# Where the first state of a chunk reads its step product, and how the first token groups are convolved

## The chip, the cores and the metric

One core of a Trainium2 chip. The engines are called by their names in the profile: PE (TensorE, with its weight loads as PEld), DVE (VectorE), ACT (ScalarE), POOL (GpSimd) and SP (SyncE, which issues the DMAs). The metric is the device time of one launch in microseconds; the time before is the median of 3 runs. All data is float32.

## The reference, cut to what matters

Two layers, each with a "conv" part and an "ffn" part. The change touches the first part alone, a two-dimensional selective scan over 4 images of 64x64 tokens with 128 channels. Four directions `k`, 256 inner channels (two halves of 128) and 16 states per channel:

```python
xc = silu(depthwise_conv3x3(xh) + conv_b)          # xh: half of x @ in_proj_w.T
xs = [x0, x1, x0 reversed, x1 reversed]            # x1: columns instead of rows
dts, Bm, Cm = split(einsum('bkdl,kcd->bkcl', xs, x_proj_weight))
delta = softplus(einsum('bkrl,kdr->bkdl', dts, dt_projs_weight) + dt_projs_bias)
...
def step(h, xs):
    ut, dt, bt, ct = xs
    dA = jnp.exp(dt[..., None] * A)
    h = dA * h + (dt * ut)[..., None] * bt[:, :, None, :]
    y = jnp.einsum('bkdn,bkn->bkd', h, ct)
    return (h, y)
```

After it come the norm, the gate and the output projection, then a mixture of experts over tokens, and a second layer with a self/row/column mixing and a spectral (FFT) convolution.

## The kernel before

**The scan.** The 4096 tokens of an image are cut into 8 chunks of 512, so there are 4 images x 4 directions x 8 = 128 chunks, and each has N = 16 states: 2048 states in all, in the loop over `s`, with `i` the chunk and `n` the state in it. For every state, channels lie on the 128 partitions, the two halves `h` behind one another:

- SP loads `bc`, the rows of B and C of that state, broadcast over the partitions, 5 states ahead (`bufs=6`).
- ACT makes `da`, the exponential of the step size times A, one instruction for each half, 3 states ahead (`bufs=5`).
- DVE multiplies the step product (step size times input) by B's row into `db[h]`, a PSUM tile of one buffer for each half, and scans: `hh = da * h + db` along the tokens.
- POOL copies the last column of `hh` to `hst`, from where the next chunk goes on, and multiplies `hh` by C's row, one state behind DVE.
- PE transposes `hh` with accumulation over the 16 states into `y`, two states behind DVE; ACT puts `y` away (`put_away`).

**The step product.** While a chunk is scanned, the generator of `step_sizes` works out the next chunk's step sizes `dl` (ACT, PE and one product on POOL) and at the end, on POOL, `dx = dl * xc`, an SBUF tile of both halves. `into_psum(i)`, called at the last state of the chunk before, has ACT copy the two halves of `dx` into `du`, one PSUM tile of one buffer with both halves. State 0 of a chunk takes its product from `dx` itself, the other 15 states take it from `du`.

**Work beside the scan.** Everything else of the images (convolutions of the next images, gates, experts) is cut into pieces that `deal` hands out between the states. A scheduler orders each engine's instructions; the traced order can be read from the built program. In it the products and scans of two neighbouring states are partly interleaved on DVE.

**The front.** `front` prepares the first image until the scan can begin. The tokens come in groups of 512 (8 rows of the image). `sums` and `spread` normalize a group, transpose it, project it on PE and put it into the padded images `xh` of each half (ACT). A 3x3 convolution reads a row above and below, so a group needs the next one. `convolve(p, h)` does a pair of groups of one half: nine taps, of which half 1 has its first `ONPE` = 5 done on PE as matmuls with diagonal weights and the last 4 on DVE, half 0 all nine on DVE. `sigmoid_of` on ACT and a product on POOL follow, and a store to `xc_d`. `rows_of` projects the groups (PE), evicts them (`sts`, ACT) and stores the rows of the step sizes, of B and of C to DRAM; `prelude` works out the first chunk's step product from `sts[0]`. Groups 0 and 1 are convolved once group 2 is spread, groups 2 and 3 after `rows_of(0)` and `prelude`.

Of the kernel before, what the change touches and what calls it, by code (L numbers as in the profile page):

```python
# [10 lines left out]
F32 = mybir.dt.float32  # L11
# [6 lines left out]
P = 128  # L18
B, H, W, C = 4, 64, 64, 128
# [9 lines left out]
SC = 512  # L29
# [7 lines left out]
BUSY = (2, 3)  # L37
XB = 6
HH = 7
ONPE = 5  # L40
AHEAD = 4

LAG = 5.0
# [64 lines left out]
def kernel(  # L108
# [35 lines left out]
    nc = tc.nc  # L144
# [144 lines left out]
    dts_d, bc_d, xc_d, xn_d, z_d, y_d = {}, {}, {}, {}, {}, {}  # L289
# [115 lines left out]
    def front(prelude):  # L405

        b = 0
# [4 lines left out]
        with tc.tile_pool(name="fr", bufs=2) as fr:  # L412
            pools = ExitStack()
            fps = pools.enter_context(tc.tile_pool(name="fr_ps", bufs=2, space=PSUM))
# [30 lines left out]
            def spread(g):  # L445
                norm_apply(x0[g], x0[g], st[g], 4)
                ps = bank([P, 4, P], "xt_ps")
                for q in range(4):
                    nc.tensor.transpose(ps[:, q, :], x0[g][:, q, :], ident)
                xn[g] = fr.tile([P, 512], F32, name="xn")  # L450
                nc.scalar.copy(xn[g], ps.rearrange("c q p -> c (q p)"))
                nc.sync.dma_start(xn_d[b][:, 512 * g : 512 * (g + 1)], xn[g])
                for h in range(2):
                    ps = bank([P, 8, W], "in_ps")
                    nc.tensor.matmul(
                        ps, w_in_t[:, h * P : (h + 1) * P], xn[g], start=True, stop=True
                    )
                    nc.scalar.copy(xh[h][:, 1 + 8 * g : 9 + 8 * g, 1 : W + 1], ps)

            def windows(h, t, r0, rows):  # L460
                dy, dx = divmod(t, 3)
                return xh[h][:, r0 + dy : r0 + dy + rows, dx : dx + W]

            def convolve(p, h):
                ps = fps.tile([P, 16, W], F32, name="fcv_ps", tag="cv")
                first = ONPE if h else 0
                for half in range(2):
                    for t in range(first):
                        nc.tensor.matmul(
                            ps[:, 8 * half : 8 * half + 8],  # L470
                            diag[:, h, t, :],
                            windows(h, t, 16 * p + 8 * half, 8),
                            start=(t == 0),
                            stop=(t == first - 1),
                        )
                for t in range(first, 9):
                    wt = cw[:, h, t : t + 1]
                    src = windows(h, t, 16 * p, 16)
                    if t == 0:
                        nc.vector.tensor_scalar(ps, src, wt, None, ALU.mult)  # L480
                    else:
                        nc.vector.scalar_tensor_tensor(ps, src, wt, ps, ALU.mult, ALU.add)
                v, e = sigmoid_of(fr, ps.rearrange("p r w -> p (r w)"), h)
                nc.gpsimd.tensor_mul(v, v, e)
                nc.sync.dma_start(xc_d[b][0, h, :, 1024 * p : 1024 * (p + 1)], v)
                for g in range(2):
                    vs[2 * p + g, h] = v[:, 512 * g : 512 * (g + 1)]

            def project(g, ps):
                for h in range(2):  # L490
                    nc.tensor.matmul(ps, xp[:, 0, h, :], vs[g, h], start=(h == 0), stop=(h == 1))
                sts[g] = fr.tile([104, SC], F32, name="xd_st", bufs=3)
                evict_soon(lambda: nc.scalar.copy(sts[g], ps))

            def rows_of(p):
                for g in range(2 * p, 2 * p + 2):
                    project(g, xps.tile([104, SC], F32, name="fxd_ps"))
                    put_bc_of(b, g, sts[g])

            for g in range(5):  # L500
                sums(g)
            for g in range(5):
                if g + 5 < 8:
                    load_x0(g + 5)
                    sums(g + 5)
                spread(g)
                if g == 2:
                    for h in range(2):
                        convolve(0, h)
            rows_of(0)  # L510
            prelude(sts[0])
            for h in range(2):
                convolve(1, h)
            rows_of(1)
            side["rows"] = AHEAD
            pools.close()
            yield None
# [63 lines left out]
    def put_bc_of(b, i, st):  # L581
        gi, c = divmod(i, NSC)
        for r0, k in ((0, gi), (64, gi + 2)):
            nc.sync.dma_start(dts_d[b][k, :, c * SC : (c + 1) * SC], st[r0 : r0 + R, :])
            for j in range(2):
                nc.sync.dma_start(
                    bc_d[b][k, c, :, j, :], st[r0 + R + j * N : r0 + R + (j + 1) * N, :]
                )
# [1295 lines left out]
    with ExitStack() as c0:  # L1884
# [100 lines left out]
        sizes = {}  # L1985

        def prelude(st):
            sizes[0] = step_sizes(0, 0, 0, st[0:R, :])
            list(sizes[0][3])
# [13 lines left out]

        def into_psum(i):

            dus[i] = bps.tile([P, 2, SC], F32, name="du")
            for h in range(2):
                nc.scalar.copy(dus[i][:, h, :], sizes[i][1][:, h, :])  # L2008

        for s in range(-5, total + 2):  # L2010
            i = max(s, 0) // N
# [23 lines left out]
            if 0 <= s < total:  # L2035
                b, k, step, _ = chunks[i]
                n = s % N
                if n == 0:
                    if i % (K * NSC) == 0:
                        y_d[b] = dram.tile([K, L, DI], F32, name=f"y_d{b}")  # L2040
                        if b > 0:
                            run(share["pieces"])
                            settle()
                        share = {"pieces": beside(b), "made": 0.0, "due": 0.0}
                    if i == len(chunks) - NSC:
                        run(share["pieces"])
                        settle()
                        kr = tc.tile_pool(name="last", bufs=1, side="right")
                        kp = kr.__enter__()
                        fin = {  # L2050
                            "stored": 0,
                            "pT": kp.tile([E, L], F32, name="pT_a"),
                            "top": kp.tile([E, P], F32, name="tops_a"),
                            "outE": kp.tile([E, C], F32, name="outE_a"),
                            "t_d": dram.tile([L, C], F32, name="t_d"),
                        }
                        share["pieces"] = after_scans(b, fin)
                        share["flow"] = True
                    hsts[i] = pb.tile([P, 2, N], F32, name="hst") if step == 0 else hsts[i - 1]
                    if i == 0:  # L2060
                        into_psum(0)
                if i < NSC and n == 0:
                    while side["rows"] < min(i + 2, NSC) or (
                        i == NSC - 1 and "columns" not in side
                    ):
                        share["made"] += next(share["pieces"])
                        tick()
                    settle()
                if i + 1 < len(chunks):
                    if n == 1:  # L2070
                        nb_, nk, _, nci = chunks[i + 1]
                        sizes[i + 1] = step_sizes(nb_, nk, nci)
                    if n >= 1:
                        next(sizes[i + 1][3], None)
                hhs[s] = pb.tile([P, 2, SC], F32, name="hh", bufs=HH)
                db = [dbs.tile([P, SC], F32, name=f"db{h}") for h in range(2)]

                src = sizes[i][1] if n == 0 else dus[i]
                for h in range(2):
                    nc.vector.tensor_mul(db[h], src[:, h, :], bcs[s][:, 0, :])  # L2080
                for h in range(2):
                    init = 0.0 if step == 0 else hsts[i][:, h, n : n + 1]
                    o, d0, d1 = hhs[s][:, h, :], das[s][:, h, :], db[h]
                    if k >= 2:
                        o, d0, d1 = o[:, ::-1], d0[:, ::-1], d1[:, ::-1]
                    i_dve = nc.vector.tensor_tensor_scan(o, d0, d1, init, ALU.mult, ALU.add)  # L2086
                for other in (acts.pop(s + 1, None), pools.pop(s + 1 - HH, None), pes.pop(s + 1 - HH, None)):
                    if other is not None:
                        tc.add_manual_dep(i_dve.ins, other, sooner, reason="waits taken early")
                if n == N - 1 and i + 1 < len(chunks):  # L2090
                    into_psum(i + 1)
# [150 lines left out]
```

## Time and profile before

| | us |
|---|---|
| median of 3 runs | 9557.68 (9557.25 to 9562.24) |
| the profiled execution's own time | 9539.45 |
| its span, first to last instruction | 9537.6 |
| first product `db` starts at | 71.16 |
| first product of the second state starts at | 82.31 |
| last scan starts at about | 7746 |

Busy over the span, from the page: DVE 8328.1 us (87%), PE 7343.6 (77%), POOL 6468.1 (68%), ACT 6137.4 (64%). The row of the page that shows DVE's busy share in 40 equal slices (a digit is a tenth, 9 is 90% or more):

```profile
DVE  8999999989999999999999999999999951566663
```

The scan is the stretch of nines. The views used below are: the busy time of each engine in a stretch; groups of instructions by line, engine and operation, with busy time, mean duration and the idle time before them with what ended it; the instructions that write or read one tile; and the timeline, in order of time, where neighbouring instructions of one kind are merged with a count and a bracket gives the idle time before and its releaser.

### The profile page before, as it was taken

The numbers are of one execution on the slowest core, as the hardware profiler recorded it, in microseconds if no ns is written. First come the engines' busy times: TensorE is split into PE (matmuls) and PEld (weight loads), VectorE is DVE, ScalarE is ACT, GpSimd is POOL, SyncE is SP. The second block draws the span as 40 slices with busy tenths as digits, with TensorE's granted clock in tenths as the row PEclk, the third lists the DMA queues.
The fourth block names the chain that finished last, engine by engine and source line by source line (L and its number), as shares of the span: only waits on it lengthen the run. The fifth ranks groups of instructions, "written<-read, shape, count | busy, mean of one in ns | idle before, by whom it ended". The sixth has DMA issues, their size and how long they took to land.

```text
span 9537.6 us, 139288 instructions
## 1 busy us (share of the span) xinstructions
PE 7343.6 (77%) x45466; PEld 4757.4 (50%) x45466; DVE 8328.1 (87%) x9161; ACT 6137.4 (64%) x11719; POOL 6468.1 (68%) x5952
## 2 busy tenths in 40 slices
PE   7687786677677777697778777767777767899997
PEld 4444444355444555454544554544555445555553
DVE  8999999989999999999999999999999951566663
ACT  6676766657755576776855677765676744555552
POOL 6787888969888888887978788978888851000000
PEclk8788787678778888798878787878887877999998
DMA  5656567668566656658757567757756663333336
GB/s 165 225 184 210 192 200 228 199 189 244 183 204 229 210 166 209 193 187 256 231 187 244 191 190 230 244 173 239 228 161 206 208 213 106 94 94 94 94 95 180
DMA packets 914666, 1806.20 MB, mean 189 GB/s; under 512 B 86784, under 2 KB 472608, under 8 KB 910232
## 3 DMA queue, kind: packets, MB, share of 16 engines
q1 hardware_dynamic: 913944, 1797.30, 59.9%
q8 instruction: 365, 5.98, 0.3%
q14 instruction: 357, 2.92, 0.1%
HBM read 1554.75 MB, written 242.22 MB: 188 GB/s over the span
## 4 chain that ended last, share of the span: by engine, by line
POOL 23%; PE 18%; issue 10%; DVE 9%; DMA 6%; ACT 6%; SPq 0%; POOLq 0%; DVEq 0%; ACTq 0%
POOL hh L2099 17%; PE sp_ps L1675 10%; DVE hh L2086 4%; DVE wt L1679 3%; PE y L2126 2%; DMA bc<-bc_d 2%; DVE db L2080 2%; ACT da L2027 2%; POOL hst L2098 1%; PE dl_ps L1941 1%; POOL ex L1935 1%; POOL dx L1944 1%; PE yk_ps L791 1%; PE fu_ps L1645 1%; ACT no_sq L353 1%
## 5 line engine op out<-in xcount | busy, mean ns | idle before, releaser
L2099 POOL TENSOR_TENSOR hh<-hh,bc 128x1024 f32<-128x1024 f32 x2048 | 4849.6, 2369 | 332.5 <-DVE hh L2086 171.8
L2086 DVE TENSOR_TENSOR_SCAN hh<-da,hst,db 128x512 f32<-128x512 f32 x3584 | 4374.9, 1258 | 129.2 <-PE y L2126 62.4
L2126 PE MATMUL y<-ident,hh 128*128 128x128 f32 x16384 | 2648.6, 315 | 1204.2 <-POOL hh L2099 1107.4
L2027 ACT ACTIVATE da<-dl,aneg 128x512 f32<-128x512 f32 x4096 | 2777.2, 718 | 1132.7 <-DVE hh L2086 1124.3
L2126 PEld LDWEIGHTS y<-ident,hh 128*128 128x128 f32 x16384 | 2212.8, 163 | 2121.7 <-POOL hh L2099 1469.2
L2080 DVE TENSOR_TENSOR db<-du,bc 128x512 f32<-128x512 f32 x3840 | 2439.6, 677 | 56.6 <-ACT du L2008 43.2
L2098 POOL COPY hst<-hh 128x2 f32<-128x2 f32 x1792 | 390.4, 218 | 674.3 <-DVE hh L2086 601.0
L1679 DVE COPY wt<-sp_ps 128x1024 f32<-128x1024 f32 x512 | 606.2, 1221 | 176.3 <-PE sp_ps L1675 153.2
L1675 PE MATMUL sp_ps<-vt,taps 32*128 32x256 f32 x8192 | 588.5, 399 | 54.7 <-DVE wt L1679 34.9
L2086 DVE TENSOR_TENSOR_SCAN hh<-da,db 128x512 f32<-128x512 f32 x512 | 594.4, 1198 | 15.8 <-PE y L2126 9.6
L1679 ACT COPY wt<-sp_ps 128x1024 f32<-128x1024 f32 x512 | 516.5, 1015 | 102.4 <-PE sp_ps L1675 82.7
L1675 PEld LDWEIGHTS sp_ps<-vt,taps 32*128 32x128 f32 x8192 | 387.8, 184 | 246.9 <-DVE wt L1679 196.6
L1679 DVE COPY zs<-sp_ps 128x1024 f32<-128x1024 f32 x128 | 156.8, 1225 | 353.0 <-PE sp_ps L1675 353.0
L1675 PE MATMUL sp_ps<-wt,ut 128*32 128x256 f32 x8192 | 448.7, 379 | 1.4 <-DVE wt L1679 1.4
L1916 PE MATMUL dt_ps<-dts,dtw 8*128 8x512 f32 x508 | 366.1, 822 | 68.4 <-ACT sg_v L400 47.0
L662 PE MATMUL cv_ps<-xh,diag 128*128 128x512 f32 x864 | 400.0, 599 | 6.2 <-ACT xh L655 3.8
L1941 PE MATMUL dl_ps<-ex,ident 128*128 128x512 f32 x512 | 309.2, 692 | 121.6 <-POOL ex L1935 121.4
L1944 POOL TENSOR_TENSOR dx<-dl,xc 128x1024 f32<-128x1024 f32 x128 | 302.6, 2364 | 90.0 <-ACT dl L1942 77.3
L1675 PEld LDWEIGHTS sp_ps<-wt,ut 128*32 128x32 f32 x8192 | 264.9, 110 | 193.6 <-issue 23.5
L1942 ACT COPY dl<-dl_ps 128x512 f32<-128x512 f32 x256 | 148.0, 578 | 327.8 <-PE dl_ps L1941 327.3
L1935 POOL TENSOR_TENSOR ex<-ex,dx 128x1024 f32<-128x1024 f32 x128 | 302.3, 2362 | 69.8 <-ACT dx L1932 66.0
L1679 ACT COPY zs<-sp_ps 128x1024 f32<-128x1024 f32 x128 | 129.5, 1012 | 320.9 <-DMA zf<-zs 161.4
(332 smaller groups left out, 9580.5 us busy)
## 6 DMA issues: line engine op xcount, KB each, us to landing
bc<-bc_d SPq DMA_DIRECT2D x2048, 512.0 KB
xc<-xc_d SPq DMA_DIRECT2D x128, 512.0 KB
y_d<-ys SPq DMA_DIRECT2D x128, 512.0 KB
w1t<-in_w_dram SPq DMA_DIRECT2D x96, 512.0 KB
w2t<-in_w_dram SPq DMA_DIRECT2D x192, 256.0 KB
yk<-y_d SPq DMA_DIRECT2D x128, 256.0 KB
yk<-y_d SPq DMA_DIRECT2D x256, 128.0 KB
zf<-zs SPq DMA_DIRECT2D x512, 64.0 KB
```

The costliest lines, as they stand in the source:

```text
L662: nc.tensor.matmul(ps, diag[:, h, t, :], xh[:, 8 * g + dy : 8 * g + dy + 8, dx : dx + W], start=(t == 0), stop=(t == 8),)
L1675: tc.keep_in_program_order(nc.tensor.matmul(*args, **kw))
L1679: tc.keep_in_program_order(copy(dst, src))
L1935: nc.gpsimd.tensor_sub(ex, ex, dx)
L1941: nc.tensor.matmul(ps, ident, t[:, h], start=t is dl, stop=t is w)
L1944: nc.gpsimd.tensor_mul(dx, dl, xc)
L2027: i_act = nc.scalar.activation(das[t][:, h, :], sizes[t // N][0][:, h, :], AF.Exp, scale=aneg[:, tk, h, t % N : t % N + 1],)
L2080: nc.vector.tensor_mul(db[h], src[:, h, :], bcs[s][:, 0, :])
L2086: i_dve = nc.vector.tensor_tensor_scan(o, d0, d1, init, ALU.mult, ALU.add)
L2098: nc.gpsimd.tensor_copy(hsts[t // N][:, :, t % N], hhs[t][:, :, last])
L2099: i_pool = nc.gpsimd.tensor_mul(hhs[t], hhs[t], bcs.pop(t)[:, 1:2, :].to_broadcast([P, 2, SC]))
L2126: i_pe = nc.tensor.matmul(ys[c][:, q, h, :], hhs[t][:, h, q * P : (q + 1) * P], ident, is_transpose=True, start=(n == 0 and k > 0 and q % ...
```

## The change

In the scan, `du` becomes two tiles, one for each half, each still of one buffer in PSUM; ACT's copies write one each, and state 0 reads them as all other states do, instead of `dx`. In the front, `convolve` takes a first group, a number of groups and the number of taps on PE: groups 0 and 1 are convolved one at a time, right after group 1 and group 2 are spread, half 0 wholly on DVE and half 1 wholly on PE; groups 2 and 3 are still a pair, both halves wholly on DVE. `rows_of` does a single group, and `prelude` follows the first.

```diff
-            def convolve(p, h):
-                ps = fps.tile([P, 16, W], F32, name="fcv_ps", tag="cv")
-                first = ONPE if h else 0
-                for half in range(2):
+            def convolve(g0, n, h, first):
+                ps = fps.tile([P, 8 * n, W], F32, name="fcv_ps", tag="cv")
+                for g in range(n):
                     for t in range(first):
                         nc.tensor.matmul(
-                            ps[:, 8 * half : 8 * half + 8],
+                            ps[:, 8 * g : 8 * g + 8],
                             diag[:, h, t, :],
-                            windows(h, t, 16 * p + 8 * half, 8),
+                            windows(h, t, 8 * (g0 + g), 8),
...
-                    src = windows(h, t, 16 * p, 16)
+                    src = windows(h, t, 8 * g0, 8 * n)
...
-                nc.sync.dma_start(xc_d[b][0, h, :, 1024 * p : 1024 * (p + 1)], v)
-                for g in range(2):
-                    vs[2 * p + g, h] = v[:, 512 * g : 512 * (g + 1)]
+                nc.sync.dma_start(xc_d[b][0, h, :, 512 * g0 : 512 * (g0 + n)], v)
+                for g in range(n):
+                    vs[g0 + g, h] = v[:, 512 * g : 512 * (g + 1)]
...
-            def rows_of(p):
-                for g in range(2 * p, 2 * p + 2):
-                    project(g, xps.tile([104, SC], F32, name="fxd_ps"))
-                    put_bc_of(b, g, sts[g])
+            def rows_of(g):
+                project(g, xps.tile([104, SC], F32, name="fxd_ps"))
+                put_bc_of(b, g, sts[g])
...
                 spread(g)
-                if g == 2:
+                if g in (1, 2):
                     for h in range(2):
-                        convolve(0, h)
-            rows_of(0)
-            prelude(sts[0])
+                        convolve(g - 1, 1, h, 9 * h)
+                if g == 2:
+                    rows_of(0)
+                    prelude(sts[0])
             for h in range(2):
-                convolve(1, h)
-            rows_of(1)
+                convolve(2, 2, h, 0)
+            for g in range(1, 4):
+                rows_of(g)
...
-            dus[i] = bps.tile([P, 2, SC], F32, name="du")
+            dus[i] = [bps.tile([P, SC], F32, name=f"du{h}") for h in range(2)]
             for h in range(2):
-                nc.scalar.copy(dus[i][:, h, :], sizes[i][1][:, h, :])
+                nc.scalar.copy(dus[i][h], sizes[i][1][:, h, :])
...
-                src = sizes[i][1] if n == 0 else dus[i]
                 for h in range(2):
-                    nc.vector.tensor_mul(db[h], src[:, h, :], bcs[s][:, 0, :])
+                    nc.vector.tensor_mul(db[h], dus[i][h], bcs[s][:, 0, :])
```

More of the change, by code (lines that the diff above doesn't have):

```diff
@@ L39 @@
 HH = 7
-ONPE = 5
 AHEAD = 4
@@ L506, in front @@
                 spread(g)
+                if g in (1, 2):
+                    for h in range(2):
+                        convolve(g - 1, 1, h, 9 * h)
                 if g == 2:
-                    for h in range(2):
-                        convolve(0, h)
-            rows_of(0)
-            prelude(sts[0])
+                    rows_of(0)
+                    prelude(sts[0])
             for h in range(2):
-                convolve(1, h)
-            rows_of(1)
+                convolve(2, 2, h, 0)
+            for g in range(1, 4):
+                rows_of(g)
             side["rows"] = AHEAD
```

## The prediction

> **What bounds the kernel now.** I read the busy time of the long middle stage first, because the shares of the whole span mix it with a tail of 1,800 us. The numbers behind each stretch are PE, PE weight loads, DVE, ACT and POOL.
>
> ```profile
> 72.00:7737.00 7665.00, 5732.04 (x26526) 3758.13 (x26526) 7439.44 (x8293) 5214.81 (x10401) 6367.06 (x5642) 0.81 0.65 207
> ```
>
> DVE is busy for 7439 of 7665 us, 97%; POOL has 83%, ACT 68%. So a microsecond that DVE computes or waits here is a microsecond of the kernel, as far as no other wait lies behind it. Next, which rows DVE spends it on (busy us, mean ns; idle before):
>
> ```profile
> L2086 DVE TENSOR_TENSOR_SCAN hh<-da,hst,db 128x512 f32<-128x512 f32 x3584 | 4374.9, 1258 | 129.2 <-PE y L2126 62.4 <-ACT da L2027 30.8 <-POOL dx L1944 6.9
> L2080 DVE TENSOR_TENSOR db<-du,bc 128x512 f32<-128x512 f32 x3840 | 2439.6, 677 | 56.6 <-ACT du L2008 43.2 <-DMA bc<-bc_d 10.4
> L2080 DVE TENSOR_TENSOR db<-dx,bc 128x512 f32<-128x512 f32 x256 | 273.3, 1098 | 2.8 <-DMA bc<-bc_d 1.3 <-POOL dx L1944 1.0
> L2008 ACT COPY du<-dx 128x512 f32<-128x512 f32 x256 | 151.1, 590 | 12.9 <-DVE db L2080 10.1 <-POOL hh L2099 1.1
> ```
>
> A state is two products `db` and two scans. The same product takes 677 ns when it reads the PSUM copy `du` and 1098 ns when it reads `dx` in SBUF, which only state 0 of a chunk does. The answer for that tile shows the spread (minimum, median, maximum ns):
>
> ```profile
> L2080 DVE TENSOR_TENSOR db<-du,bc x3840: 660/676/715, 82.3 to 7744.2; 128x512 f32<-128x512 f32 x192
> ...
> L2080 DVE TENSOR_TENSOR db<-dx,bc x256: 661/687/2856, 71.2 to 7687.7; 128x512 f32<-128x512 f32 x128
> ```
>
> So the price is not of the size: half of the `dx` rows are as quick as the others, the rest up to four times as long. The timeline of one chunk's first state shows what they meet (start, duration; DVE, then POOL):
>
> ```profile
> 1161.81 1.59 DVE L2080 TENSOR_TENSOR db<-dx,bc 128x512 f32<-128x512 f32 x1
> 1163.32 2.44 DVE L2086 TENSOR_TENSOR_SCAN hh<-da,hst,db 128x512 f32<-128x512 f32 x2
> 1165.68 2.15 DVE L2080 TENSOR_TENSOR db<-dx,bc 128x512 f32<-128x512 f32 x1
> ```
>
> ```profile
> 1160.47 2.38 POOL L2099 TENSOR_TENSOR hh<-hh,bc 128x1024 f32<-128x1024 f32 x1
> 1164.64 0.19 POOL L2098 COPY hst<-hh 128x2 f32<-128x2 f32 x1 [1.80 <-DVE hh L2086]
> 1164.91 2.36 POOL L2099 TENSOR_TENSOR hh<-hh,bc 128x1024 f32<-128x1024 f32 x1
> ```
>
> POOL's product ends at 1162.85 and 1167.27; the `dx` rows end at 1163.40 and 1167.83, 0.55 us later each time. They wait for POOL to finish and then run. A `du` row that starts under a POOL product never does (maximum 715 ns of 3840).
>
> Last, when ACT writes the copy. At another boundary (DVE, then ACT):
>
> ```profile
> 3265.80 1.55 DVE L2080 TENSOR_TENSOR db<-dx,bc 128x512 f32<-128x512 f32 x2
> 3267.27 2.44 DVE L2086 TENSOR_TENSOR_SCAN hh<-da,hst,db 128x512 f32<-128x512 f32 x2
> ```
>
> ```profile
> 3264.59 1.06 ACT L1930 ACTIVATE w<-ex 128x1024 f32<-128x1024 f32 x1
> 3265.55 2.55 ACT L2027 ACTIVATE da<-dl,aneg 128x512 f32<-128x512 f32 x4
> 3268.00 1.21 ACT L2008 COPY du<-dx 128x512 f32<-128x512 f32 x2
> ```
>
> The copy starts 2.2 us after state 0 began, and nobody minds: state 1 needs it at 3269.6. After the change state 0 itself needs it.
>
> **The change part by part.** *State 0 reads the copy.* I went through the 127 boundaries after the first chunk. At 63 a `dx` row is over 0.1 us longer than 0.69 us; together 106 us too long. This goes: **-106 us**. The bounds are nothing (rival D) and -108 us (256 x (1098 - 677) ns).
>
> *The wait for the copy at state 1.* DVE waited 43.2 us for it, 4.0 of them in the first chunk; the wait moves ahead to state 0 and is counted there anew: **-39 us**.
>
> *The wait for the copy at state 0.* Each half's copy is released by its own product of state 15; from there to state 0's product of that half DVE does one more product and two scans, 0.68 + 2.44 = 3.1 us, and the copy takes 0.59 us. So if ACT is free there is no wait. But ACT is in order. For each boundary I took the ACT instruction that stands directly ahead of each copy in the built order of the changed kernel (often two `da` exponentials earlier than before), looked up the end of the same instruction in this trace, and added 0.66 us (copy and signal). At 3265.80 that gives 2.3 + 0.66, a wait of 2.9 us. At 79 boundaries the copy is in time; at 48 it is late, by 166 us in all: 6 under 1 us, 26 of 1 to 3.5, 13 of 3.5 to 8, and 3 above 8 with 37 us (DVE waits there before, too). For five boundaries, where that instruction has a far-off place in the old order, I kept the old predecessor. **+166 us**. Bounds: 37 us, if ACT is late only at those three; 226 us, if at each of the 48 two more `da` rows (1.24 us) stand ahead. I take 166, since it is read boundary by boundary. Behind the waiting copy ACT holds `da` of three states on, whose scans come 10 us later, and ACT idles 1,100 us of the stage waiting for scans anyway: its own wait costs nothing.
>
> *What later waits do with it.* Where DVE loses time at a boundary but waits for others (PE `y`, `bc`, ACT) later in that chunk, the loss shrinks the wait: chunk by chunk at most 36 us. Where it gains and waits later, the gain is lost: at most 30 us. Together **-6 us**.
>
> *The front.* Before, the second state starts at 82.3 us:
>
> ```profile
> 68.86 1.29 DVE L482 SCALAR_TENSOR_TENSOR fcv_ps<-xh,cw,fcv_ps 128x1024 f32<-128x1024 f32 x1 [17.48 <-PE fcv_ps L469]
> ...
> 77.06 1.21 DVE L2086 TENSOR_TENSOR_SCAN hh<-da,db 128x512 f32<-128x512 f32 x1
> 82.31 1.30 DVE L2080 TENSOR_TENSOR db<-du,bc 128x512 f32<-128x512 f32 x2 [4.04 <-ACT du L2008]
> ```
>
> DVE waited 17.5 us for PE's taps. In the new order PE does all nine taps of half 1 of group 0 (0.89 us each, 5.32 us for six, so 8 us) after group 1's projection, to 27 us; sigmoid on ACT to 30; then two taps, group 2's projection, seven taps and the projection of `xd`, to 41.6. ACT reads `dt` at 44; its chain (10 us in the trace) with `ex` on POOL (2.35 us) and the remaining `xh` copies woven in gives DVE `xh` of group 3 at 51 and of group 4 at 59. DVE's 18 taps over groups 2 and 3, 1.17 us apart, with half 1 waiting for its copy, end at 73. ACT then has three 1.0 us functions ahead of `du0` and one more ahead of `du1`; the second state starts at about 79.4: **-3 us**. The 18 narrow taps, a size without a row (between 0.59 us, half a wide one, and 0.75 us, L1842), lie in DVE's idle time. SP issues six stores of `xc` for four and POOL four products of 1.3 us for two of 2.35; neither waits on them. Bounds -10 and +6 us, by a group's taps either way.
>
> **Sum:** -106 - 39 + 166 - 6 - 3 = +12 us on the profiled execution's 9539.45 us (span 9537.6). That execution lies 18 us under the median of the runs; put on 9557.68 the sum gives **about 9570 us**, no change that can be told: two medians of this kernel are told apart from about 0.2%, 19 us.
>
> **Rivals.** *B, ACT is in time.* The new order was made with the copies needed early; if ACT's lag is half of what the old trace shows, the wait is 83 and the sum -71 us: 9487 us; if only the three big ones stay, -117: 9441 us. For it: ACT is only 68% busy. Against: the lags are ACT rows that stay ahead of the copy in the new order.
>
> *C, the copy becomes the bound of each boundary (the other side).* DVE, quicker by 106 us, comes to ACT's queue sooner, and at the 226 us end the sum is +72: 9630 us; if also half of the 63 boundaries that were slowed by POOL turn late by the typical 2.5 us, +150: 9708 us. It is slower than before from a total wait of about 154 us. For it: at 48 boundaries ACT is already behind; against: at the others the median lead is about 3 us.
>
> *D, it doesn't do what it says.* The long rows would belong to the place (state 0, both engines at a chunk's start), not to the source; then -106 falls out: +118, 9676 us. Against: 3840 `du` rows with no long one.
>
> The Trainium skill, "SBUF — State Buffer", section "SBUF: two separate sides", speaks to D: VectorE and GpSimd share a pair of ports as an exclusive lock, taken by a VectorE instruction with two SBUF inputs against a GpSimd one that reads SBUF, and the loser blocks for the whole instruction. By that rule all the long rows go; the 0.55 us tails above agree.
>
> **How the numbers follow.** The forecast has 0.47 with a range of its own of 9530 to 9610 (half of the wait's upper step, the front's bounds); of it 0.08 falls below 9538.6, 0.27 within 0.2%, 0.12 above 9576.8. B has 0.27, nearly all of it faster; C 0.22 and D 0.04, slower. That is faster 0.34, same 0.28, slower 0.38. The range that leaves out a tenth on each side goes from 9475, in the middle of B, to 9640, past C's first number.
>
> **What would show it.** No `db` row over 0.72 us and no `dx` source in DVE's rows; a DVE wait for ACT's `du` of about 166 us at some 48 boundaries (under 80: B; over 230: C); the median state still 3.54 us; second state near 79 us. Wrong if the stage from the first state to 7737 changes for another cause than these two: more DVE idle on PE `y` or ACT `da`.

## The result, and the profile after

The median of the changed kernel is 9506.87 us (six runs, 9497.18 to 9514.12), that of the kernel before 9557.47 us in the runs beside it (six, 9554.17 to 9562.92). The ratio is 0.9945, with an interval of 0.9932 to 0.9958: faster by 0.55%, or 50.6 us. The forecast of 9570 us, no change, was wrong in its direction; the time lies inside the stated range of 9475 to 9640.

The profiled executions differ by less: the spans are 9537.6 and 9505.2 us, 32.4 apart. The profiled execution of before lay 18 us under its median, that of after (9507.07) on it. So 32 us can be accounted for row by row, and the other 18 are the scatter of single executions: all runs of the kernel before in this study lie between 9536 and 9572 us.

The busy time of the engines (PE, weight loads, DVE, ACT, POOL; then the clock, the DMA share and GB/s) from the second state's start to the last scan's end, in after:

```profile
85.60:7710.70 7625.10, 5718.48 (x26554) 3749.82 (x26553) 7336.01 (x8300) 5212.42 (x10406) 6280.06 (x5652) 0.81 0.65 208
```

The same stretch of before:

```profile
82.30:7747.30 7665.00, 5735.03 (x26558) 3762.44 (x26557) 7443.44 (x8298) 5213.58 (x10408) 6373.90 (x5650) 0.81 0.65 207
```

DVE's busy column falls by 107.4 us, yet the stretch only by 39.9; granted clock (0.81) and DMA share (0.65) are the same. The second state starts 3.3 us later than before, and what follows the last scan takes 4.2 us longer. -39.9 + 3.3 + 4.2 is the -32.4 us of the spans. Where the other 67.5 us of DVE's gain went is seen in the group of products of after (busy us, mean ns; idle before, with what ended it):

```profile
L2078 DVE TENSOR_TENSOR db<-du,bc 128x512 f32<-128x512 f32 x4096 | 2605.0, 677 | 149.6 <-ACT du L2007 128.3 <-DMA bc<-bc_d 18.1
```

All 4096 products have the short price of 677 ns; the rows with `dx` as their source are gone. Their wait for ACT's copy has grown from 43.2 to 128.3 us. No product is long any more (minimum, median, maximum ns of the products by their tile):

```profile
L2078 DVE TENSOR_TENSOR db<-du,bc x4096: 660/676/703, 83.2 to 7707.7; 128x512 f32<-128x512 f32 x196
```

DVE's waits in the scan (us in total, times, longest), after and then before:

```profile
DVE db L2078 <- ACT du L2007: 128.3, 50, 13.5
...
DVE hh L2084 <- PE y L2124: 64.1, 35, 5.9
...
DVE hh L2084 <- ACT da L2026: 20.4, 15, 3.6
```

```profile
DVE hh L2086 <- PE y L2126: 72.1, 33, 10.3
...
DVE db L2080 <- ACT du L2008: 43.2, 14, 11.6
DVE hh L2086 <- ACT da L2027: 34.2, 24, 2.9
```

The copy takes over as the largest wait of the scan; the two others shrink by 22 us together. One boundary at which it is late, DVE and then ACT:

```profile
2837.99 2.43 DVE L2084 TENSOR_TENSOR_SCAN hh<-da,hst,db 128x512 f32<-128x512 f32 x2
2843.32 1.30 DVE L2078 TENSOR_TENSOR db<-du,bc 128x512 f32<-128x512 f32 x2 [2.90 <-ACT du L2007]
```

```profile
2835.98 0.69 ACT L1919 ACTIVATE ex<-dt_ps,dtb 128x512 f32<-128x512 f32 x1 [8.35 <-PE dt_ps L1915]
2836.57 0.68 ACT L1920 ACTIVATE dl<-dt_ps,dtb 128x512 f32<-128x512 f32 x1
2837.14 1.06 ACT L1927 ACTIVATE ex<-ex 128x1024 f32<-128x1024 f32 x1
2838.08 1.33 ACT L2026 ACTIVATE da<-dl,aneg 128x512 f32<-128x512 f32 x2
2839.31 1.05 ACT L1929 ACTIVATE w<-ex 128x1024 f32<-128x1024 f32 x1
2840.26 2.55 ACT L2026 ACTIVATE da<-dl,aneg 128x512 f32<-128x512 f32 x4
2842.71 1.10 ACT L2007 COPY du<-dx 128x512 f32<-128x512 f32 x2
```

ACT stands idle for 8.35 us at an instruction that waits for PE, then works off 6.7 us of queue, and only then makes the copy; DVE, done at 2840.42, starts again at 2843.32. This is the usual case. Of the 49 such waits after the first chunk (124.6 us), 41 that stand behind an ACT that had been idle for over 0.8 us at a stretch in the 14 us ahead of its copy make 98.6 us, and the 8 behind an ACT without such a stretch 26.0 us. What ACT idled for last is mostly PE (62 us of the waits, most of it `dt_ps` 17, `ar_ps` 15 and `pk_ps` 9), POOL's `no_m` (17) and one transfer (13).

### The profile page after: what moved, and what is told of

The parts are those of the page before. It is cut to its first block, busy times and chain, and to the rows that moved or that the text cites. A ratio compares the mean times of both kernels' runs of the same rounds, so it can differ in the third digit from the quotient of the medians.

```text
span 9505.2 us, 139568 instructions
## 1 busy us (share of the span) xinstructions
PE 7331.8 (77%) x45462; PEld 4748.2 (50%) x45462; DVE 8222.5 (87%) x9171; ACT 6138.1 (65%) x11727; POOL 6373.1 (67%) x5954
## 4 chain that ended last, share of the span: by engine, by line
POOL 23%; PE 20%; issue 11%; DVE 10%; ACT 7%; DMA 6%; SPq 0%; POOLq 0%; DVEq 0%; ACTq 0%
POOL hh L2097 17%; PE sp_ps L1674 10%; DVE hh L2084 4%; DVE wt L1678 3%; PE y L2124 3%; ACT da L2026 2%; DVE db L2078 2%; DMA bc<-bc_d 1%; POOL hst L2096 1%; PE dl_ps L1940 1%; POOL dx L1943 1%; POOL ex L1934 1%; ACT no_sq L352 1%; DMA yk<-y_d 1%; PE yk_ps L790 1%
## 5 line engine op out<-in xcount | busy, mean ns | idle before, releaser
L2078 DVE TENSOR_TENSOR db<-du,bc 128x512 f32<-128x512 f32 x4096 | 2605.0, 677 | 149.6 <-ACT du L2007 128.3
L2096 POOL COPY hst<-hh 128x2 f32<-128x2 f32 x1792 | 336.6, 188 | 695.6 <-DVE hh L2084 629.1
```

The lines of the kernel that those rows point to most:

```text
L2078: nc.vector.tensor_mul(db[h], dus[i][h], bcs[s][:, 0, :])
L2096: nc.gpsimd.tensor_copy(hsts[t // N][:, :, t % N], hhs[t][:, :, last])
```

## The experiments

All kernels below compute the whole reference. The first four ran beside 21 runs of the kernel before (median 9555.17 us), the last three beside nine (9556.46). The times are read as ratios to those.

**1. The change in the scan alone** (two tiles, read by every state; the old front):

```diff
-            dus[i] = bps.tile([P, 2, SC], F32, name="du")
+            dus[i] = [bps.tile([P, SC], F32, name=f"du{h}") for h in range(2)]
...
-                nc.scalar.copy(dus[i][:, h, :], sizes[i][1][:, h, :])
+                nc.scalar.copy(dus[i][h], sizes[i][1][:, h, :])
...
-                src = sizes[i][1] if n == 0 else dus[i]
-                    nc.vector.tensor_mul(db[h], src[:, h, :], bcs[s][:, 0, :])
+                    nc.vector.tensor_mul(db[h], dus[i][h], bcs[s][:, 0, :])
```

> The change in the scan alone, with the front as before. Theory S (the source: products of state 0 no longer wait for POOL, -106 us; the wait for the copy rises by 85 us; other waits of DVE fall by some 20 us): the second state starts at about 82 us as before, no db row over 0.72 us, DVE waits for du some 120 us, and the time is 3 us under the changed kernel, about 9504 us. Rival F (the front brings a good part of it): 9530 us or more.

Measured 9506.34 us, ratio 0.9955 (0.9943 to 0.9968). Its wait for the copy is that of after:

```profile
DVE db L2079 <- ACT du L2008: 132.5, 51, 14.6
```

The scan's edits bring the whole gain. The waits come back in another program and execution at nearly the same size, so they are no scatter of single runs.

**2. The change of the front alone** (the main added lines; what they replace stands in the change above):

```diff
+            def convolve(g0, n, h, first):
...
+                if g in (1, 2):
+                    for h in range(2):
+                        convolve(g - 1, 1, h, 9 * h)
+                if g == 2:
+                    rows_of(0)
+                    prelude(sts[0])
             for h in range(2):
+                convolve(2, 2, h, 0)
+            for g in range(1, 4):
+                rows_of(g)
```

> The change in the front alone, the scan as before. Theory S: the second state starts at 85 to 86 us (82.3 before), the db rows from dx keep about 106 us too much, 9558 to 9563 us. Rival F: 9530 us or less. Rival O (a new order of instructions shakes the time by tens of us whatever the edit): outside of 9545 to 9575 us.

Measured 9552.72 us, ratio 0.9996 (0.9987 to 1.0005): no change that can be told. The second state starts at 83.8 us, beside 82.3 in before and 85 to 86 expected.

**3. One tile for the copy, read by every state** (the changed kernel with the old tile):

```diff
-            dus[i] = [bps.tile([P, SC], F32, name=f"du{h}") for h in range(2)]
+            dus[i] = bps.tile([P, 2, SC], F32, name="du")
...
-                nc.scalar.copy(dus[i][h], sizes[i][1][:, h, :])
+                nc.scalar.copy(dus[i][:, h, :], sizes[i][1][:, h, :])
...
-                    nc.vector.tensor_mul(db[h], dus[i][h], bcs[s][:, 0, :])
+                    nc.vector.tensor_mul(db[h], dus[i][:, h, :], bcs[s][:, 0, :])
```

> The changed kernel with du as one tile of both halves again, read by every state. Theory S: the long db rows stay away (-106 us), but the copy of half 0 is released by the product of half 1 of state 15, which in the chunks with interleaved states (some 45 of 128) stands directly ahead of state 0's product: about 0.7 us more wait in each, 30 us, so 9530 to 9545 us and a du wait of 150 to 170 us. Rival T (two tiles matter little, since it is ACT that is late): within 8 us of the changed kernel, 9500 to 9515 us.

Measured 9602.43 us, ratio 1.0049 (1.0037 to 1.0062): slower than before, and 96 us over the changed kernel. Both theories missed it. DVE's waits for the copy (us in total, times, longest):

```profile
DVE db L2078 <- ACT du L2007: 229.7, 82, 13.8
```

A boundary, DVE and then ACT:

```profile
1157.70 0.67 DVE L2078 TENSOR_TENSOR db<-du,bc 128x512 f32<-128x512 f32 x1
1159.71 0.70 DVE L2078 TENSOR_TENSOR db<-du,bc 128x512 f32<-128x512 f32 x1 [1.33 <-ACT du L2007]
```

```profile
1158.47 1.21 ACT L2007 COPY du<-dx 128x512 f32<-128x512 f32 x2 [0.48 <-DVE db L2078]
```

ACT is free, having stood idle for 0.48 us, but its first copy starts only after the last product of state 15 (1158.37), and the first product of state 0 only after the second copy (1159.68). With one tile and one buffer the two halves are freed and filled together, so here even a punctual ACT costs 1.3 us. This boundary shows the mechanism bare, but its kind is rare: in this kernel a product of state 15 stands directly ahead of state 0's on DVE at 3 of the 127 boundaries after the first chunk (about 36 in the changed kernel), at nearly all others a scan. The filling can be read at all of them: at each of the 81 waits after the first chunk DVE starts 0.03 us after the end of the second copy, and 80 of their 224.5 us lie behind the end of the first; in the changed kernel it is 1.3 of the 105.5 us at state 0's first product. By this reading the filling makes most of the 101 us by which the wait grew. The rest, the later freeing and the other order of DVE's and ACT's instructions that came with one tile, was not tried apart.

**4. Two tiles, but state 0 reads `dx`** (the changed kernel with the old source):

```diff
-                    nc.vector.tensor_mul(db[h], dus[i][h], bcs[s][:, 0, :])
+                    src = sizes[i][1][:, h, :] if n == 0 else dus[i][h]
+                    nc.vector.tensor_mul(db[h], src, bcs[s][:, 0, :])
```

> The changed kernel, but state 0 reads dx in SBUF again; the two tiles and the front stay. Theory S: the waits for POOL are back (db from dx 1000 to 1150 ns in the mean), the du wait falls to 30 to 50 us, 9550 to 9570 us. Rival O or T (the gain is of the tiles or of the order): 9505 to 9530 us.

Measured 9538.71 us, ratio 0.9986 (0.9977 to 0.9995), between the ranges of the two theories (9550 to 9570 and 9505 to 9530). The groups of products:

```profile
L2079 DVE TENSOR_TENSOR db<-du,bc 128x512 f32<-128x512 f32 x3840 | 2446.1, 678 | 29.7 <-ACT du L2007 18.5 <-DMA bc<-bc_d 7.9
L2079 DVE TENSOR_TENSOR db<-dx,bc 128x512 f32<-128x512 f32 x256 | 290.1, 1163 | 2.4 <-DMA bc<-bc_d 2.0
```

The long rows are back (1163 ns), and the wait at state 1 is 18.5 us where experiment 2, with one tile, has 50.4. Two tiles alone are worth some 14 us (9552.72 to 9538.71; the wait falls by 32 us, but DVE is busy for 17 us more, with longer `dx` rows), and reading the copy at state 0 another 32 (9538.71 to 9506.87).

**5. The copies first in ACT's queue.** Experiment 1, with every ACT instruction that the program issues after the copies, up to state 2 of the next chunk, ordered behind them:

```diff
+        def behind_copies():
+            for ins in traced[copied["from"] :]:
+                if ins.engine == copied["last"].ins.engine:
+                    tc.add_manual_dep(ins, copied["last"].ins.name, order, reason="queued behind")
+            copied["from"] = len(traced)
...
-                nc.scalar.copy(dus[i][h], sizes[i][1][:, h, :])
+                copied["last"] = nc.scalar.copy(dus[i][h], sizes[i][1][:, h, :])
+            copied["from"] = len(traced)
...
+            if 0 < s < total and s % N in (0, 1, 2, N - 1) and "last" in copied:
+                behind_copies()
...
```

The last two lines stand in the loop twice, behind POOL's part of a state and at its end.

> The change in the scan alone (old front), and every ACT instruction that the program issues after the copies, up to state 2 of the next chunk, is ordered behind them. Theory H (the copy is late because ACT's queue holds, ahead of it, work of the next chunk or dealt pieces that themselves wait for PE): the du wait falls from 132 us to 40 to 90 us, other waits grow a little since that work comes later, 9440 to 9490 us. Rival L (ACT simply has too much work around the boundary): the du wait stays over 110 us, 9495 to 9520 us.

Measured 9478.23 us (9468.65 to 9480.37), ratio 0.9917 (0.9904 to 0.9931): faster than both kernels, 28 us under experiment 1. Its waits:

```profile
DVE db L2088 <- ACT du L2016: 111.5, 38, 11.9
...
DVE hh L2094 <- PE y L2136: 70.7, 35, 6.9
...
DVE hh L2094 <- ACT da L2036: 16.8, 15, 2.6
```

The wait for the copy falls by 21 us against experiment 1, those for `y` and `da` by 6 and 10; all of DVE's idle time in the scan falls from 309.7 to 272.0 us, and the stretch by as much (7642.4 to 7604.0). That is 38 us and not 28, since the profiled execution of experiment 1 (9520.33) is the slowest of its five. So ACT's order does set a part of the wait. But 111.5 us is above the 40 to 90 expected, and what rival L gave for the wait (over 110); the time is theory H's (9440 to 9490). After the first chunk 36 us of it stand behind an ACT that is busy throughout, and 17 behind ACT's `y`, which waits for POOL's `no_m`. The edit moves only what the program issues after the copies; what it issues ahead of them still stands ahead. Whether that is all of the rest wasn't tried.

**6. The same, and no side work dealt out at state 14:**

```diff
-BUSY = (2, 3)
+BUSY = (2, 3, 14)
```

> As the last, and no piece of the work beside is dealt out in state 14 (it is spread over the 13 other states). Theory H: pieces that wait for PE no longer stand ahead of the copy, du wait under 50 us, 9420 to 9470 us unless the denser pieces make waits on PE y elsewhere (64 us in the changed kernel). Rival L: as the last, 9495 to 9520 us.

Measured 9477.51 us (9466.38 to 9491.83), ratio 0.9923 (0.9910 to 0.9936): as experiment 5.

```profile
DVE hh L2094 <- PE y L2136: 103.7, 44, 8.4
DVE db L2088 <- ACT du L2016: 81.4, 27, 13.8
```

The wait for the copy gives up another 30 us, the wait for PE's `y` takes 33 and that for `da` 10 (27.2). What is gained at one wait is lost at others, and neither the wait (under 50) nor the time (9420 to 9470) of theory H is reached.

**7. State 1 also reads `dx`** (the kernel before):

```diff
-                src = sizes[i][1] if n == 0 else dus[i]
+                src = sizes[i][1] if n <= 1 else dus[i]
```

> The kernel before, with states 0 and 1 reading dx in SBUF. Theory S (a product that reads SBUF twice waits for POOL): the excess of the dx rows over 0.69 us goes from 106 us over 256 rows to 180 to 230 us over 512 rows, the du wait of 43 us goes to under 15 us, 9595 to 9640 us. Rival P (the long rows belong to the place, the first state): state 1's dx rows are not long, the sum stays near 106 us, and the time falls by the du wait, 9515 to 9535 us.

Measured 9674.52 us, ratio 1.0129 (1.0115 to 1.0143).

```profile
L2080 DVE TENSOR_TENSOR db<-du,bc 128x512 f32<-128x512 f32 x3584 | 2282.0, 679 | 26.9 <-DMA bc<-bc_d 14.3 <-ACT du L2008 8.8
L2080 DVE TENSOR_TENSOR db<-dx,bc 128x512 f32<-128x512 f32 x512 | 565.0, 1139 | 7.7 <-DMA bc<-bc_d 6.1 <-POOL dx L1944 1.0
```

Twice the rows have twice the price: 512 at a mean of 1139 ns. What they exceed 0.69 us by adds up to 228.8 us, as expected, and DVE's busy time over the span rises by 138 us (8328.1 to 8466.4). The wait for the copy falls to 8.8 us, but other waits fill its place (idle time in the scan 220.7 us beside 226.6), which is the main reason that the time is above the 9595 to 9640 expected.

## Why the prediction went wrong

**The long rows (-106 us): right.** DVE's busy time fell by 107.4 us, no product is over 0.703 us, and experiments 4 and 7 bring the long rows back with their source and double them with it. Rival D, place and not source, falls: in experiment 7 the `dx` rows of state 1 have a mean of 1115 ns, those of state 0 1163.

**The wait for the copy (-39 + 166 us): the step that failed, by its size.** The mechanism is there, and so is the count (44 boundaries with a wait, 48 foretold), but the waits add up to 124.6 us. With the old wait gone the net is +85 us instead of +127, and these 42 us are nearly all of the 44 between the +12 forecast and the -32.4 found; the other terms were off by 1 to 13 us, but about cancel. The three big ones were right (37.1 us foretold, 33.8 measured), and so were the last six chunks: 15.9 foretold, 13.5 measured. Eight others, 24.8 us together, came to 0.2, two in neighbouring chunks among them (44 and 45: 4.3 and 2.3 us foretold, none seen). The remaining difference is on smaller waits that came out shorter, less 4 us at boundaries where none was foretold.

The step said: "looked up the end of the same instruction in this trace". It carries an instruction's lag over from the old order as if it belonged to the instruction. But most of these lags are ACT standing still for another engine and then working off its queue, so they can depend on when PE, POOL or a transfer delivers relative to DVE. At chunk 44 the old trace has ACT begin `ex` on `dt_ps` 0.8 us ahead of state 0 and the copy 2.6 us after it; in after the same `ex` begins 5.3 us ahead, and the copy 0.9 us ahead. The built order of ACT shows what stands ahead of the copy, not when it runs. Experiment 5 shows that the order itself has a price: with the instructions issued later kept behind the copies, 21 us of the wait go. At two more boundaries without a wait, chunks 31 and 79, it was the place itself that changed. In before the copy of half 0 starts 4.4 and 2.8 us after state 0's first product, in after 9.1 and 2.8 us ahead of it, in front of the rows that it stood behind before. The step kept the old predecessor at five boundaries, these two probably among them: a redo from the two traces gives them some 9 of the 24.8 us by the old predecessor, and no wait for half 0 by the new one.

Why the rest of the lags shrank stays open. It isn't only that ACT waited: in the same redo (171 us in all, beside the 166) the 11 boundaries at which ACT had had no idle stretch over 0.8 us in before go from 45 us foretold to 28 found, the 41 at which it had stood for PE or POOL from 115 to 92.

**What later waits absorb (-6 us): too small.** DVE's other idle time in the scan fell by 19 us: 22 less for `y` and `da`, 3 more elsewhere. Experiment 6 shows the same exchange the other way round. These terms leave 1 us of the stretch open. The sum had no term for what follows the last scan (+4.2 us).

**The front (-3 us): +3.3 us, inside its bounds.** The taps of groups 2 and 3 were to end at 73 us, and the second state to start at 79.4. In after:

```profile
54.55 1.29 DVE L478 TENSOR_SCALAR fcv_ps<-xh,cw 128x1024 f32<-128x1024 f32 x1 [15.35 <-ACT xh L457]
...
62.23 1.29 DVE L478 TENSOR_SCALAR fcv_ps<-xh,cw 128x1024 f32<-128x1024 f32 x1 [2.42 <-ACT xh L457]
...
83.15 0.70 DVE L2078 TENSOR_TENSOR db<-du,bc 128x512 f32<-128x512 f32 x1 [3.68 <-ACT du L2007]
...
85.02 1.27 DVE L2078 TENSOR_TENSOR db<-du,bc 128x512 f32<-128x512 f32 x2
```

The taps begin at 54.55 us after a wait for ACT's `xh`, wait for it again ahead of half 1, and run to 79.5 (the last row of 13 taps starts at 63.43 and lasts 16.05). That is 6.5 us after the forecast, and the second state at 85.6 is 6.2 after it. Some 3.5 us of that is when ACT's copies `xh` come (the taps go on at 54.55 and 62.23 us, foretold 51 and 59); the rest lies behind the second wait, where 14 taps in 17.3 us still stood and the forecast had left 14 us. The three functions ahead of the copy are as foretold. Experiments 1 and 2 agree that the front is worth nothing that can be told.

**The base.** The forecast put a sum made on the profiled execution on a median 18 us above it. That execution lay near the low end of its kernel's runs; the changed kernel's lay on its median. Of the 63 us between 9570 and 9507, 44 are the sum and 18 this.

**The rivals.** B, ACT half as late (a wait of 83 us, 9487 us), and the forecast (166 us) lie about equally far from the 124.6 us found. B's direction was right. C, the copy as the bound of each boundary from a wait of about 154 us, did not come with the change, but experiment 3 is that case: 229.7 us of waiting, and slower than before.

## What to carry to other kernels

When a queue in program order makes the data that another engine waits for, a lag read from the old trace tells where the waits will be better than how long they are: here 44 boundaries came for 48 foretold, but the total was a third too large. A sum in which two such terms nearly cancel should carry that uncertainty in its direction too. And a handover buffer of two halves should be two tiles, with the copies ahead of work that nobody waits for: the first was worth 96 us here where every state reads the copy (14 where state 0 does not), the second 28.

## What the runs showed of the hardware

The wait between DVE and POOL goes both ways. Of the `dx` products of before, all 90 that are longer than 0.79 us started under a row of POOL and ended 0.55 to 0.56 us after that row's end, as did all 183 in experiment 7; of the `du` products of after, some 3000 started under a row of POOL that had 0.1 us or more to go, and none was long. But when DVE is first, POOL pays. In before, DVE and then POOL:

```profile
3039.33 1.27 DVE L2080 TENSOR_TENSOR db<-dx,bc 128x512 f32<-128x512 f32 x2
```

```profile
3036.05 0.19 POOL L2098 COPY hst<-hh 128x2 f32<-128x2 f32 x1 [0.80 <-DMA bc<-bc_d]
...
3039.47 1.17 POOL L2098 COPY hst<-hh 128x2 f32<-128x2 f32 x1 [0.79 <-DVE hh L2086]
```

The same copy of two columns takes 0.19 us alone and 1.17 us under two `dx` products, ending with them (3040.64 and 3040.60). In before 78 of the 1792 copies take over 0.3 us, in after none, and the mean falls from 218 ns to 188. The group in after:

```profile
L2096 POOL COPY hst<-hh 128x2 f32<-128x2 f32 x1792 | 336.6, 188 | 695.6 <-DVE hh L2084 629.1 <-DMA bc<-bc_d 18.3 <-DVE hard L953 6.4
```

So reading the copy in PSUM also took 54 us off POOL's busy time. The Trainium skill, "SBUF — State Buffer", section "SBUF: two separate sides", speaks of an exclusive lock on the shared ports at which the loser blocks; both directions here agree with it, with 0.98 us as the price that POOL paid at this copy.
